# Gated cross-attention: three small regroupings of vector work, in the first quad, in every softmax and in the last two rows of tiles

## The chip, the cores and the metric

The kernel runs on one core of one Trainium2 chip. The metric is the device time of one execution in microseconds (us). The time before is 961.03 us, the median of three runs (960.99, 961.03 and 962.22).

## The reference, cut to what matters

```
memory_proj    = memory @ W_mem.T                               # (8, 64, 1024)
scores         = hidden @ memory_proj.T / sqrt(1024)            # (8, 1024, 64)
attn           = softmax(scores)
memory_context = attn @ memory_proj
gate           = sigmoid(concat(hidden, memory_context) @ W_gate.T + b_gate)
fused          = hidden + gate * memory_context
out            = fused * rsqrt(mean(fused**2) + 1e-6) * norm_w
```

Everything is float32. `hidden` is 8 x 1024 x 1024, `memory` 8 x 64 x 512, `W_gate` 1024 x 2048. The product of `hidden` with its half of `W_gate` is by far the largest piece of arithmetic.

## The kernel before, in words

**Tiling.** The 8192 rows of `hidden` are cut into 16 quads (`q`) of 512 rows; a quad is four tiles of 128 rows (`t` = 0 to 3), and each tile has two halves of 512 columns (`h` = 0, 1). Tiles 0 and 1 form row 0, tiles 2 and 3 row 1. The gate product of a quad is a two-level Strassen-like scheme: seven outer products, in `ORDER` 1, 6, 7, 5, 4, 2, 3 (the number is `o` in the code), and in each of them seven inner products. Their PSUM banks are named af, ed, kB and kC; VectorE and GpSimd add the partial sums (`u2`, `u3`, `u4`, and the "gate" tiles `O[q, t]`). The left operands need sums too: GpSimd makes them in `inner_s` (tile "l").

**Weights.** The right operands of each outer product need four sums of their own, T1, T2, R12 and T4 (`inner_sum`, tile "it"). Those of products 2 and 3 are made only once, by VectorE, within the first quad.

**Order of the work.** Everything is kept in program order on each engine. A quad has 49 slots, one per inner product. `at(slot, fn, ...)` hangs a piece of work on a slot, and `step()` issues it ahead of that slot's product; `mid((q, o), ...)` and `mid((q, o, 0), ...)` hang work in the middle of an outer product, behind and ahead of the sums that follow its visit. So each engine's queue is an order written out by hand.

**Visits.** After the third inner product of products 4 and 3 (`second` in the code), `visit` issues 32 matrix instructions for the memory half of the gate of two outer products at once, and for the attention context (tile "pc"). It takes over the banks "b" and "c", in which kB and kC had just been, so TensorE can begin only when VectorE has read kB (into `u2`) and kC (into `u3`) of the same outer product. Then `fin_af` and `fin_ed` complete the gate sums, ScalarE takes the sigmoid, and `gated` multiplies with the context.

**Softmax.** `softmax_a` (slot 10 of each quad) takes the row maximum on VectorE (L429), multiplies it there by -1/32 (L430), and ScalarE takes four exponentials (L435).

**The last quad.** There the residual comes from SBUF: `last_gated` multiplies (gate<-gate,pc) and adds `hidden` (gate<-gate,xl), `last_square` takes each half's sum of squares on ScalarE, `last_root` the square root, and `last_norm` a reciprocal (L761), one VectorE instruction that multiplies a half by the reciprocal and by `norm_w` (L765), and the store of that half from SyncE's queue (L767). `sqrt_table` loads ScalarE's table for the root ahead of need. With `slot` standing at 770 after product 4 and at 784 after product 3, the tiles of row 1 have their roots at slots 773 and 774, tile 3 its two halves at 775 and 776, tile 2 its first half in the middle of product 3 and its second at 781; all of row 0 comes after slot 784, in the order root of tile 1, root of tile 0, tile 1's halves, tile 0's halves.

Line 92 is the helper of all matmuls, line 95 that of all two-input sums, on VectorE or on GpSimd; line 98 that of SyncE's DMAs.

Of the kernel before, what the change touches and what calls it, by code (L numbers as in the profile page):

```python
# [9 lines left out]
AF = mybir.ActivationFunctionType  # L10
ALU = mybir.AluOpType
# [9 lines left out]
def tile_gated_cross_attention_rmsnorm(  # L21
# [42 lines left out]
    nc = tc.nc  # L64
# [4 lines left out]
    NQ = B * QPB  # L69
# [3 lines left out]
    H = 512  # L73
    C = 256
    NPAIR = BM // P
    SCALE = 1.0 / float(D) ** 0.5
# [12 lines left out]
    pin = tc.keep_in_program_order  # L89
# [4 lines left out]
    def tt(eng, o, a, b, op):  # L94
        pin(eng.tensor_tensor(o, a, b, op))  # L95

    def load(o, i):
        pin(nc.sync.dma_start(o, i))

    def t4k(pool, shape, tag, name):  # L100
        return pool.tile(shape, F32, tag=tag, name=name)
# [31 lines left out]
    for k in range(KD):  # L133
        t = t4k(*((gpool, [P, D], "gate") if k < 7 else (apool, [P, D], "s4")), f"w2_{k}")
# [8 lines left out]
    nw_sb = const.tile([P, D], F32, name="nw_sb")  # L143
# [194 lines left out]
    A, S, L2, O = {}, {}, {}, {}  # L338
    sTs, attns, attnTs, scs, dens, mps, mgs = {}, {}, {}, {}, {}, {}, {}
    def where(q, t=0):  # L340
        return q // QPB, (q % QPB) * QT + t * P
# [84 lines left out]
    def softmax_a(q):  # L426
        sc = scs.pop(q)
        mx = t4k(small, [P, 4], "mx", f"mx{q}")
        pin(nc.vector.tensor_reduce(mx, sc, AX.X, ALU.max))  # L429
        pin(nc.vector.tensor_scalar(mx, mx, -SCALE, None, ALU.mult))  # L430
        e = attns[q] = t4k(small, [P, 4, M], "e", f"e{q}")
        den = dens[q] = t4k(small, [P, 4], "den", f"den{q}")
        for t in range(4):
            pin(
                nc.scalar.activation(  # L435
                    e[:, t], sc[:, t], AF.Exp, bias=mx[:, t : t + 1], scale=SCALE, accum_out=den[:, t : t + 1]
                )
            )
# [167 lines left out]
    def at(slot, fn, *args):  # L606
        due.setdefault(slot, []).append(lambda: fn(*args))

    def mid(key, fn, *args):
        beside.setdefault(key, []).append(lambda: fn(*args))  # L610
# [5 lines left out]
    def plan(q):  # L616
# [11 lines left out]
        at(t0 + (11 if q else 22), outer_s, q, 4)  # L628
        at(t0 + 9, transpose_scores, q)
        at(t0 + 10, softmax_a, q)  # L630
        at(t0 + 13, softmax_b, q)
        at(t0 + 18, transpose_attn, q)
# [20 lines left out]
    for o in (2, 3):  # L653
        w1_place(o)
    for i, (o, n) in enumerate((o, n) for o in (2, 3) for n in range(4)):
        at((3, 4, 5, 6, 12, 14, 16, 18)[i], inner_sum, nc.vector, o, n)
    slot = 0

    def step():
        nonlocal slot  # L660
        for fn in due.pop(slot, ()):
            fn()
# [5 lines left out]
    def sigmoid(q, t, h):  # L668
        g = O[q, t][:, h * H : (h + 1) * H]
        pin(nc.scalar.activation(g, g, AF.Sigmoid))  # L670
# [77 lines left out]
    def last_root(t):  # L748
# [5 lines left out]
            )  # L754
        )

    def last_norm(t, h):
        b, n0 = where(NQ - 1, t)
        rstd = halves[t][0][:, 2:3]
        if h == 0:  # L760
            pin(nc.vector.reciprocal(rstd, rstd))  # L761
        cols = slice(h * H, (h + 1) * H)
        g = O[NQ - 1, t][:, cols]
        pin(
            nc.vector.scalar_tensor_tensor(g, g, rstd, nw_sb[:, cols], ALU.mult, ALU.mult)  # L765
        )
        load(out[b, n0 : n0 + P, cols], g)  # L767

    def sqrt_table():

        t = t4k(small, [P, 1], "warm", "warm")
        pin(nc.scalar.activation(t, eps_sb, AF.Sqrt))
# [75 lines left out]
    def gate(q, t, h, pc, w):  # L848
        sigmoid(q, t, h)
        if q + 1 == NQ:  # L850
            at(slot + w, last_gated, t, h, pc)
        else:
            at(slot + w, gated, q, t, h, pc)

    def outer_product(q, o):
# [4 lines left out]
        nxt = q + 1 < NQ  # L860
# [5 lines left out]
        def product(out, lhsT, s, start):  # L866
            nonlocal slot
            for k in range(2):
                mm(out, lhsT[:, k, :], w_op(o, s)[:, k, :], start and k == 0, k == 1)
            slot += 1  # L870
# [51 lines left out]
        if second:  # L922
            row, h, _ = EXT[o]
            gate(q, 2 * row + 1, h, pcs[1], 2 if o == 3 and not nxt else 1)
        step()
        product(af[:, 1], s4, R22, False)
        step()
# [8 lines left out]
        if second and not nxt:  # L936
            c, d = 2 * row, 2 * row + 1
            if o == 3:
                sqrt_table()
            when = (3, 4, 5, 6, None, 11) if o == 4 else (0, 2, 2, 2, 3, 3)  # L940
            at(slot + when[0], last_root, d)
            at(slot + when[1], last_root, c)
            for w_, (t, h_) in zip(when[2:], ((d, 0), (d, 1), (c, 0), (c, 1))):
                if w_ is None:
                    mid((q, 3, 0), last_norm, t, h_)
                else:
                    at(slot + w_, last_norm, t, h_)
        elif second:

            c, d = 2 * row, 2 * row + 1  # L950
            for t in (d, c):
                at(slot + 5, residual, q, t)
            if row == 0:
                when = (17, 18, -1, None, 33, -2) if q + 2 < NQ else (17, 18, 20, 22, 24, 25)
            else:
                when = (17, 18, 22, 24, 29, 31)
            at(slot + when[0], square, q, c)
            at(slot + when[1], square, q, d)
            for w_, (t, h_) in zip(when[2:], ((c, 0), (c, 1), (d, 0), (d, 1))):
                if w_ is None:  # L960
                    mid((q + 1, 4), norm, q, t, h_)
                elif w_ < 0:
                    mid((q + 1, 4, 0) if w_ == -1 else (q + 1, 3), norm, q, t, h_)
                else:
                    at(slot + w_, norm, q, t, h_)
        del L2[q, o]

    for q in range(NQ):
        plan(q)
        for o in ORDER:  # L970
            outer_product(q, o)
# [29 lines left out]
```

## Time and profile before

| What | Value |
|---|---|
| median of the three runs | 961.03 us |
| the profiled execution's own time | 961.78 us |
| its span in the trace | 960.0 us |
| granted TensorE clock, mean | 0.997 |
| last matrix instruction starts / span ends | 947.67 us (four of them) / 960.0 us |
| TensorE idle for VectorE's u sums, whole span | 2.2 + 0.5 + 0.2 us |
| last four stores issued at | 954.37, 955.12, 955.93 and 956.59 us |

The page gives busy time by engine. The view of waits says for whom an engine sat idle. The timeline lists instructions: start and duration in us, engine, line, operation, output and inputs with shapes, and in brackets the idle time just before and what ended it. Positions such as 941.33 are us from the span's start. The profiled execution took 0.75 us longer than the median, and its own time is 1.78 us longer than its span, so a difference is worked out on the span and then taken from either.

### The profile page before, as it was taken

To read this page: it belongs to the slowest core of one execution; us is meant where nothing else is said; L and a number is where in the kernel's file an instruction comes from. 1 tells how busy PE (TensorE), PEld (TensorE's weight loads), DVE (VectorE), ACT (ScalarE), POOL (GpSimd) and SP (SyncE) were. 2 spreads that over 40 slices of the span, in tenths; PEclk is the share of its full clock that TensorE was granted. 3 is DMA by queue.
4 is the path that set the end of the run, shared out by engine and by line. 5 is a ranking of instruction groups with operands and counts; after the bars stand their busy time and mean duration, and the time that the engine had idled before them with its cause. 6 is when DMAs were issued, how large, how long until landed. Compare 5 with 4: busy or idle time off the path is not lost.

```text
span 960.0 us, 14298 instructions
## 1 busy us (share of the span) xinstructions
PE 944.4 (98%) x4984; PEld 777.6 (81%) x4984; DVE 817.3 (85%) x1260; ACT 366.3 (38%) x779; POOL 712.2 (74%) x778
## 2 busy tenths in 40 slices
PE   9999999999999999999999999999999999999994
PEld 7546788888888888888888888888888888888883
DVE  6989878888888888988888888988888888978887
ACT  3000335262433535262433535262433525262454
POOL 4997867788677777787677777777677877777681
PEclk9999999999999999999999999999999999999998
DMA  9866674481919365481919365481919365481712
GB/s 378 268 153 155 108 126 106 104 182 44 209 45 189 91 141 118 109 177 43 210 45 189 88 142 120 101 185 40 213 45 187 87 145 121 107 180 40 203 66 89
DMA packets 70919, 128.33 MB, mean 134 GB/s; under 512 B 12352, under 2 KB 49216, under 8 KB 70592
## 3 DMA queue, kind: packets, MB, share of 16 engines
q1 hardware_dynamic: 61664, 93.86, 37.0%
q0 software_dynamic: 9184, 33.56, 19.1%
q8 instruction: 40, 0.66, 0.3%
q14 instruction: 31, 0.25, 0.1%
HBM read 87.56 MB, written 41.68 MB: 135 GB/s over the span
## 4 chain that ended last, share of the span: by engine, by line
PE 92%; DVE 4%; ACT 1%; issue 1%; POOL 1%; DMA 1%; SPq 0%; POOLq 0%; DVEq 0%; ACTq 0%
PE af L92 28%; PE ed L92 19%; PE pc L92 11%; PE kC L92 9%; PE kB L92 9%; PE psT L92 6%; PE pg L92 5%; PE pm L92 2%; DVE gate L95 1%; DVE u L95 1%; DMA wm<-in_w_mem_t 1%; POOL l L95 0%; DVE gate L765 0%; DVE gate L699 0%; PE sc L420 0%
## 5 line engine op out<-in xcount | busy, mean ns | idle before, releaser
L95 POOL TENSOR_TENSOR gate<-gate,u 128x512 f32<-128x512 f32 (+1 forms) x224 | 248.9, 1123 | 193.9 <-DVE u L95 180.0
L670 ACT ACTIVATE gate<-gate 128x512 f32<-128x512 f32 x128 | 79.8, 630 | 184.2 <-DVE gate L95 184.2
L352 DVE STREAM_TRANSPOSE a<-xq 128x512 f32<-128x512 f32 x128 | 141.0, 1105 | 3.3 <-POOL it L95 3.3
L95 POOL TENSOR_TENSOR l<-a 128x256 f32<-128x256 f32 x128 | 111.9, 874 | 18.7 <-PE af L92 17.5
L699 DVE SCALAR_TENSOR_TENSOR gate<-gate,ss,nw_sb 128x512 f32<-128x512 f32 x120 | 120.7, 1007 | 1.1
L92 PE MATMUL pc<-mg,attnT 64*128 64x256 f32 x512 | 119.0, 383 | 2.2 <-DVE u L95 2.2
L92 PE MATMUL kB<-it,l 128*128 128x256 f32 x448 | 115.1, 379 | 0.5 <-DVE u L95 0.5
L92 PE MATMUL ed<-it,l 128*128 128x256 f32 x448 | 115.0, 379 | 0.0
L92 PEld LDWEIGHTS pc<-mg,attnT 64*128 64x128 f32 x512 | 93.2, 187 | 22.9 <-DVE u L95 13.0
L876 ACT COPY u<-af 128x256 f32<-128x256 f32 x112 | 40.7, 363 | 185.6 <-PE af L92 185.2
L95 DVE TENSOR_TENSOR gate<-gate,pc 128x512 f32<-128x512 f32 x113 | 76.0, 683 | 33.2 <-ACT gate L670 33.1
L92 PE MATMUL af<-w,a 128*128 128x256 f32 x384 | 98.5, 379 | 0.0
L92 PEld LDWEIGHTS kB<-it,l 128*128 128x128 f32 x448 | 85.1, 190 | 12.3 <-issue 0.8
L92 PEld LDWEIGHTS ed<-it,l 128*128 128x128 f32 x448 | 83.9, 190 | 10.7
L95 DVE TENSOR_TENSOR gate<-gate,ed 128x512 f32<-128x512 f32 x112 | 76.1, 680 | 14.4 <-POOL gate L95 14.3
L95 POOL TENSOR_TENSOR l<-s 128x256 f32<-128x256 f32 x96 | 85.1, 886 | 3.0 <-PE af L92 3.0
L92 PEld LDWEIGHTS af<-w,a 128*128 128x128 f32 x384 | 73.0, 190 | 10.3 <-issue 0.5
L95 DVE TENSOR_TENSOR gate<-gate,af 128x512 f32<-128x512 f32 (+1 forms) x128 | 76.0, 604 | 2.1 <-POOL gate L95 1.4
L92 PE MATMUL af<-mg,attnT 64*128 64x256 f32 x256 | 68.8, 389 | 0.0
L92 PE MATMUL ed<-it,a 128*128 128x256 f32 x256 | 67.4, 386 | 0.0
L684 ACT ACTIVATE junk<-gate 128x1024 f32<-128x1024 f32 x60 | 63.5, 1058 | 6.9 <-DMA gate<-in_x 6.0
L92 PE MATMUL af<-t,s 128*128 128x256 f32 x256 | 65.8, 380 | 0.0
(138 smaller groups left out, 1993.5 us busy)
## 6 DMA issues: line engine op xcount, KB each, us to landing
xq<-in_x SPq DMA_DIRECT2D x64, 512.0 KB, 10.4
gate<-in_x POOLq DMA_DIRECT2D x60, 512.0 KB, 8.5
out<-gate SPq DMA_DIRECT2D x60, 512.0 KB, 3.4
w<-in_w_gate_t SPq DMA_DIRECT2D x8, 512.0 KB, 10.2
w<-in_w_gate_t SPq DMA_DIRECT2D x2, 2048.0 KB, 16.1
mg<-mgd SPq DMA_DIRECT2D x16, 256.0 KB, 5.9
wm<-in_w_mem_t SPq DMA_DIRECT2D x4, 512.0 KB, 6.4
mpd<-mpT SPq DMA_DIRECT2D x4, 512.0 KB, 7.0
```

What stands on the lines that cost most here:

```text
L92: pin(nc.tensor.matmul(o, lhsT, rhs, start=start, stop=stop, skip_group_check=True))
L95: pin(eng.tensor_tensor(o, a, b, op))
L352: nc.vector.transpose(A[key][:, :, r * P : (r + 1) * P], chunks(xq[q][:, 4 * t : 4 * t + 4, :], KD)[:, half * KH : (half + 1) * KH],)
L670: pin(nc.scalar.activation(g, g, AF.Sigmoid))
L684: nc.scalar.activation(junk, O[q, t], AF.Square, accum_out=ss[:, t % 2 : t % 2 + 1])
L699: nc.vector.scalar_tensor_tensor(g[:, cols], g[:, cols], rstd[:, t % 2 : t % 2 + 1], nw_sb[:, cols], ALU.mult, ALU.mult,)
L876: pin(nc.scalar.copy(p1, af[:, 0]))
```

## The change

1. In every quad, the product of the row maximum with -1/32 goes from VectorE to ScalarE, just ahead of the exponentials.
2. In the first quad, the four weight sums of outer product 3 go from slots 12, 14, 16 and 18 to the middle of product 4 (two of them, behind the gate sums of its visit), slot 33 and slot 35. Those of product 2 stay at 3 to 6.
3. In the last quad, tile 2 is multiplied by `norm_w` on GpSimd (`last_weigh`, both halves, issued in the middle of product 3), and by the reciprocal on ScalarE (slots 780 and 781). Tile 3 keeps its VectorE instructions, at slot 774 (its first half, now ahead of `u4` of product 2) and in the middle of product 3 (its second half).
4. The first halves of tiles 0 and 1 are also multiplied by `norm_w` on GpSimd, behind the last `pre` sum, and by the reciprocal on ScalarE. Their second halves stay on VectorE.

```
-        pin(nc.vector.tensor_scalar(mx, mx, -SCALE, None, ALU.mult))
+        pin(nc.scalar.activation(mx, mx, AF.Copy, scale=-SCALE))
...
-        at((3, 4, 5, 6, 12, 14, 16, 18)[i], inner_sum, nc.vector, o, n)
+        if i in (4, 5):
+            mid((0, 4), inner_sum, nc.vector, o, n)
+        else:
+            at((3, 4, 5, 6, None, None, 33, 35)[i], inner_sum, nc.vector, o, n)
...
+    def last_weigh(t, h):
+        cols = slice(h * H, (h + 1) * H)
+        g = O[NQ - 1, t][:, cols]
+        tt(nc.gpsimd, g, g, nw_sb[:, cols], ALU.mult)
...
-        pin(
-            nc.vector.scalar_tensor_tensor(g, g, rstd, nw_sb[:, cols], ALU.mult, ALU.mult)
-        )
+        if t == 2 or t < 2 and h == 0:
+            pin(nc.scalar.activation(g, g, AF.Copy, scale=rstd))
+        else:
+            pin(
+                nc.vector.scalar_tensor_tensor(g, g, rstd, nw_sb[:, cols], ALU.mult, ALU.mult)
+            )
         load(out[b, n0 : n0 + P, cols], g)
...
             gate(q, 2 * row + 1, h, pcs[1], 2 if o == 3 and not nxt else 1)
+            if o == 3 and not nxt:
+                for t in range(2):
+                    last_weigh(t, 0)
...
-            when = (3, 4, 5, 6, None, 11) if o == 4 else (0, 2, 2, 2, 3, 3)
+            when = (3, 4, 4, None, 10, 11) if o == 4 else (0, 2, 2, 2, 3, 3)
+            if o == 4:
+                for h_ in range(2):
+                    mid((q, 3, 0), last_weigh, c, h_)
```

## The prediction, made before the change was run

> **What bounds the kernel now.** I read the page's busy times first, then TensorE's waits, then the timeline around each wait and behind the last matrix instruction.
>
> ```profile
> PE 944.4 (98%) x4984; PEld 777.6 (81%) x4984; DVE 817.3 (85%) x1260; ACT 366.3 (38%) x779; POOL 712.2 (74%) x778
> PE pc L92 <- DVE u L95: 2.2, 3, 1.4
> PE kB L92 <- DVE u L95: 0.5, 1, 0.5
> PE kC L92 <- DVE u L95: 0.2, 1, 0.2
> ```
>
> TensorE is busy 98% of the span, and in all 16 quads it waits for VectorE five times. So a change to vector work can only win at those five places and behind the last matmul. Three of the five lie in the first quad:
>
> ```profile
> 109.87 1.10 PE L92 MATMUL kB<-it,l 128*128 128x256 f32 x4 [0.45 <-DVE u L95]
> 111.19 1.10 PE L92 MATMUL kC<-t,l 128*128 128x256 f32 x4 [0.21 <-DVE u L95]
> 112.75 0.48 PE L92 MATMUL pc<-mg,attnT 64*128 64x256 f32 x1 [0.46 <-DVE u L95]
> 93.63 2.23 DVE L430 TENSOR_SCALAR mx<-mx 128x4 f32<-128x4 f32 x1
> 96.70 0.84 DVE L95 TENSOR_TENSOR it<-w 128x512 f32<-128x512 f32 x1
> 103.01 0.69 DVE L95 TENSOR_TENSOR gate<-gate,ed 128x512 f32<-128x512 f32 x1 [1.51 <-POOL gate L95]
> ```
>
> The reader is to see VectorE falling behind from 93 us on: a four-column multiply that takes 2.23 us, then the weight sums, then a gate sum at 103.01 that waits for a late GpSimd. The brackets understate the loss. From af of product 4 (its last matmul group ahead of kB, 108.40) to the visit (112.75) are 4.35 us; the same stretch of product 3, without a wait, is 128.69 - 126.00 = 2.69. **The first quad loses 1.66 us.** The same subtraction in the last quad: product 4, 923.94 - 920.85 = 3.09, a loss of 0.40; product 3, 941.33 - 937.20 = 4.13, a loss of 1.44.
>
> ```profile
> 941.33 0.48 PE L92 MATMUL pc<-mg,attnT 64*128 64x256 f32 x1 [1.38 <-DVE u L95]
> 938.36 1.45 DVE L765 SCALAR_TENSOR_TENSOR gate<-gate,halves,nw_sb 128x512 f32<-128x512 f32 x1
> 941.88 1.27 POOL L95 TENSOR_TENSOR gate<-gate,u 128x512 f32<-128x512 f32 x1 [1.48 <-DVE halves L761]
> 941.91 1.79 DVE L765 SCALAR_TENSOR_TENSOR gate<-gate,halves,nw_sb 128x512 f32<-128x512 f32 x1
> 950.87 0.69 DVE L95 TENSOR_TENSOR gate<-gate,xl 128x512 f32<-128x512 f32 x1
> 954.00 0.29 ACT L752 ACTIVATE halves<-halves 128x1 f32<-128x1 f32 x1
> 955.78 0.74 DVE L765 SCALAR_TENSOR_TENSOR gate<-gate,halves,nw_sb 128x512 f32<-128x512 f32 x1
> 956.59 0.33 SPq L98 DMA_DIRECT2D out<-gate  x1
> ```
>
> Two normalising instructions stand in VectorE's queue ahead of u2, on which the last visit waits. The one at 941.91 began 0.03 us behind GpSimd's sum and took 1.79 us instead of 0.75: it ended 0.55 us after GpSimd did. So **a VectorE instruction with two SBUF inputs and a GpSimd sum exclude each other**; the one that is waiting goes next. Sums with a PSUM input keep their 0.68 us beside GpSimd (927.21). Behind the last matmul VectorE works without a pause to 956.52, and the last store, issued at 956.59, ends the span at 960.0. The four last stores move 1.05 MB from 955.2 to 958.2 at up to 385 GB/s; issued together they would need some 2.75 us.
>
> **What the Trainium skill says.** GPSIMD Engine Reference, section 8 (Key points), says that GpSimd shares its SBUF interfaces with VectorE and collides with instructions that have two SBUF inputs; the 1.79 us above agrees. The same page, section 3.1, gives some 2.6 cycles per element for a two-input GpSimd operation: my estimate for 512 columns is 512 x 2.6 / 1.2 GHz = 1.11 us, and the trace's 128x512 sums take 1.19 (back to back) to 1.27 us. ScalarE: Activation LUTs, section "Table sets: the hidden batching unit", says that a copy is in every set; the trace agrees, L876's copies run behind sigmoids, exponentials and roots without a table load. So the moved multiplies bring no load.
>
> **The change, part by part.**
>
> *Multiply of the maximum, to ScalarE.* VectorE loses 16 instructions of 0.78 us (906.74) or, in the first quad, 2.23. ScalarE gains 16 of about 0.3 us (its 128x1 operations take 0.29) in a place where it waits for the maximum anyway. In the last quad the exponentials then start some 0.55 us sooner, the reciprocal at 910.22 (which waited 0.64 for them) too, so GpSimd's and VectorE's chain up to u2 of product 4 (923.48) is about 0.6 ahead, and the loss of 0.40 goes: I take **0.35**. In the 14 quads between, TensorE waited for nothing, so it is worth nothing there; its cover is TensorE's own work.
>
> *Weight sums of product 3.* Slots 12 to 18 lose 0.84 + 0.68 + 0.69 + 0.89 = 3.10 us of VectorE, and GpSimd's left-operand sums beside them (1.17 to 1.27 us each) fall back to 0.73. Following the queue: u4 of product 7 is then ruled by TensorE (101.1), GpSimd's gate sum is done before it, and the sum of 103.01 starts at about 101.1, a lead of 1.9 us. With it u2 of product 5 is at 107.4 instead of 109.31, u3 at 108.9, and u2 of product 4 ends at about 111.0, just in time for the unstalled visit at 112.75 - 1.66 = 111.09. The same 3.1 us come back between 114 and 123 us, where VectorE has 0.43 + 0.27 + 0.69 + 0.70 us of idle time and starts 1.9 ahead; u2 of product 3 then ends within 0.2 us of the visit that needs it. Unknown is what each sum pays for colliding with GpSimd: 0.69 (no collision) to 1.84 (the worst row of a two-input instruction, 928.53). The four took 3.10 beside a busy GpSimd before, so I take that. Of 1.66 us I take **1.45**, with 0 and 1.66 as ends (TensorE is busy from there on, so what is won is kept).
>
> *Row 1 of the last quad.* u3 of product 2 stays at 937.50. The reciprocal follows at 937.83 and tile 3's first half at 938.03, 0.03 behind GpSimd's sum of 938.00, so it pays 1.79 again and ends at 939.8; u4 follows at 939.73, u2 at 940.06 to 940.47, and the visit starts at 940.53 instead of 941.33: 0.80 us of 1.44 (1.33 if VectorE came first). Tile 3's second half follows u3 (940.91) ahead of GpSimd's sum, at 0.75 us, which delays that sum to 942.75. Behind it are queued the two multiplies of tile 2, up to 943.94 and 945.13. The add of tile 0's first half (due at 944.05) waits for the second one and ends at 945.68, against 946.40 before. ScalarE's two scalings of tile 2 (0.62 each, the sigmoid's 0.61 to 0.63) fall in gaps at 944.0 and 946.7; the one removed from VectorE at 946.32 gives another 0.66. The last fin_af is at 948.18 instead of 949.55.
>
> *Row 0.* GpSimd's last gate sum ends at 948.14; its multiplies of tiles 0 and 1 run to 949.33 and 950.52. The add of tile 1's second half (due at 949.51, 950.87 before) waits for the second and ends at 951.05; tile 0's add ends at 952.38 (952.88 before). Square and root of tile 0 follow to 953.45, and only then, in ScalarE's order, come the scalings of tile 1 (953.97) and tile 0 (954.5); VectorE does the other two halves by 954.44. So the first store goes at 954.0 instead of 954.37, and, being first in SyncE's queue, it holds the others. They follow at 0.35 to 0.45 us each instead of 0.75, so the 1.05 MB need about 2.75 instead of 3.05 us. Row 0 and 1 together: 0.37 + 0.3 to 0.5, I take **0.75**. Ends: a multiply in GpSimd has no row in this trace; 1.19 (the sum's) is the floor, 2.4 (twice that) the ceiling I allow; if the adds escape both locks, 1.75.
>
> *Sum*: 0.35 + 1.45 + 0.75 = 2.55 us. The profiled execution's 961.78 becomes 959.2 (span 957.4), and the median 961.03 becomes **958.5**.
>
> **The rivals.** (a) *The first quad's loss is only moved*: the sums collide at slots 31 to 35 and hold u2 back at product 3's visit, or the lead is less than 1.2 us. Against it speaks the idle time listed above, for it the 0.2 us of slack. Then 0.35 + 0.75 remain: 959.9. (b) *The locks miss*: the adds at 944.05 and 949.51 get in ahead of GpSimd. 1.45 + 0.35 + 1.75 = 3.55: 957.5. For it: an order decided by hundredths; against: GpSimd's pairs are back to back. (c) *GpSimd's multiply is slow*, the one that ends slower than before. At 2.4 us each, tile 2's second multiply runs to about 948.1 and holds the add of tile 1's first half; fin_af comes at 949.85, tile 0's multiply to 952.2 and tile 1's to 955.15 hold the last two adds, and the first store goes at 957.4, 3.0 late. With 0.4 back from the stores and 1.8 from the other parts: 961.03 + 0.8 = 961.8. The first store moves by (3.0 + 0.37) / 1.2 = 2.8 us for each us of the multiply, so it turns slower from about 2.1 us per multiply. For it: no multiply of GpSimd in the trace; against: the skill's price is set by reading two inputs, which a sum pays too. With (a) on top it is 963.3.
>
> **How the numbers follow.** About 0.2% (1.9 us) is what a measurement here tells from no change; 959.1 and 962.95 are the bounds. Forecast 0.58 (own range 957.9 to 959.4; 0.50 of it below 959.1), (a) 0.20 (same), (b) 0.12 (faster), (c) 0.10 (0.06 slower, 0.04 same). Faster 0.62, same 0.32, slower 0.06. The range 957.2 to 960.3 takes in the forecast, (b) and (a), and leaves (c) out.
>
> **What would show it.** Right: no wait of TensorE for u between 100 and 130 us, none at product 4 of the last quad, some 0.6 us left at the last visit; GpSimd's multiplies at 1.2 us; one 1.2 to 1.8 us add in each of the two last rows; the last four stores issued within about 1.4 us. Wrong: a new wait at product 3's visit in the first quad, GpSimd multiplies near 2 us, or stores that still go one by one.

## The result and the profile after

The changed kernel takes 958.77 us (median of seven runs, 958.32 to 960.52) against 961.25 us before (median of seven): 2.5 us less, ratio 0.9974 with a 95% interval of 0.9964 to 0.9984. The prediction was 958.5. The profiled execution took 958.62 us with a span of 956.8, against 961.78 and 960.0 before: 3.2 us less, 0.7 more than the medians differ by. Where that 0.7 comes from is part of the story below.

The page's first row and TensorE's waits for VectorE's sums, after the change (us in total, times, longest):

```profile
PE 943.8 (99%) x4984; PEld 778.1 (81%) x4984; DVE 810.7 (85%) x1240; ACT 372.4 (39%) x799; POOL 719.7 (75%) x782
PE pc L92 <- DVE u L95: 0.3, 1, 0.3
```

Of five waits one is left. (A "visit" below is its first matrix instruction, the `pc<-mg,attnT` line; a bracket on it is a wait.) The timeline says which. First quad, after:

```profile
101.16 0.68 DVE L95 TENSOR_TENSOR gate<-gate,ed 128x512 f32<-128x512 f32 x1
107.43 0.42 DVE L95 TENSOR_TENSOR u<-u,kB 128x256 f32<-128x256 f32 x1
111.07 0.48 PE L92 MATMUL pc<-mg,attnT 64*128 64x256 f32 x1
114.94 0.90 DVE L95 TENSOR_TENSOR it<-w 128x512 f32<-128x512 f32 x1
115.88 1.10 DVE L95 TENSOR_TENSOR it<-w,it 128x512 f32<-128x512 f32 x1
126.40 0.39 DVE L95 TENSOR_TENSOR u<-u,kB 128x256 f32<-128x256 f32 x1
127.01 0.48 PE L92 MATMUL pc<-mg,attnT 64*128 64x256 f32 x1
```

The visit of product 4 starts at 111.07 instead of 112.75, without a bracket. Product 7's kB, which starts at 103.21 (103.22 before), is 7.86 us ahead of it instead of 9.53. The late weight sums (114.94, 115.88, and two more at 119.02 and 121.00 of 0.84 and 0.81 us) cost 3.65 us, and u2 of product 3 ends at 126.79, 0.2 us ahead of the visit that needs it.

The last quad, after: the softmax's first sum, the gate sum behind it, the visit of product 4, and then tile 2's add beside GpSimd's sum:

```profile
905.04 1.96 DVE L95 TENSOR_TENSOR s<-a,s 128x1024 f32<-128x1024 f32 x1
908.00 0.18 DVE L442 RECIPROCAL den<-den 128x4 f32<-128x4 f32 x1
913.25 0.69 DVE L95 TENSOR_TENSOR gate<-gate,ed 128x512 f32<-128x512 f32 x1 [1.13 <-POOL gate L95]
922.32 0.48 PE L92 MATMUL pc<-mg,attnT 64*128 64x256 f32 x1 [0.30 <-DVE u L95]
926.90 0.69 DVE L95 TENSOR_TENSOR gate<-gate,xl 128x512 f32<-128x512 f32 x1
926.92 1.80 POOL L95 TENSOR_TENSOR gate<-gate,u 128x512 f32<-128x512 f32 x1
938.25 0.48 PE L92 MATMUL pc<-mg,attnT 64*128 64x256 f32 x1
```

The wait that is left (0.30) is the one that I had struck out. Tile 2's add came 0.02 us ahead of GpSimd's sum here and won (0.69 us). In the first trace of before it had come 0.01 us ahead too, and lost:

```profile
928.53 1.84 DVE L95 TENSOR_TENSOR gate<-gate,xl 128x512 f32<-128x512 f32 x1
928.54 1.27 POOL L95 TENSOR_TENSOR gate<-gate,u 128x512 f32<-128x512 f32 x1
```

The starts in the trace don't tell who has the turn. That is some 0.8 us between these two profiles which no edit made (shown below), and with it the last visit (938.25) does not wait at all.

The end, after:

```profile
941.68 0.69 DVE L95 TENSOR_TENSOR gate<-gate,xl 128x512 f32<-128x512 f32 x1
943.00 1.05 DVE L95 TENSOR_TENSOR gate<-gate,xl 128x512 f32<-128x512 f32 x1
947.06 1.13 DVE L95 TENSOR_TENSOR gate<-gate,xl 128x512 f32<-128x512 f32 x1
950.30 0.29 ACT L755 ACTIVATE halves<-halves 128x1 f32<-128x1 f32 x1
950.50 1.32 ACT L773 ACTIVATE gate<-gate,halves 128x512 f32<-128x512 f32 x2
950.82 0.75 DVE L776 SCALAR_TENSOR_TENSOR gate<-gate,halves,nw_sb 128x512 f32<-128x512 f32 x1
951.23 0.33 SPq L98 DMA_DIRECT2D out<-gate  x1
```

The add of tile 0's first half (941.68) got in ahead of GpSimd and waited for nothing, where I had it wait 1.1 us; the add behind it (943.00) was held instead, for 1.05 us against 0.69 before. The add of tile 1's second half (947.06) was held, as forecast. The two scalings of ScalarE come behind tile 0's root, and the first of the last four stores goes at 951.23. From the last visit to that store are 12.98 us (13.04 before), and from it to the end 5.57 (5.63 before).

### The profile page after: what moved, and what is told of

The parts are those of the page before. It is cut to its first block, busy times and chain, and to the rows that moved or that the text cites. A ratio compares the mean times of both kernels' runs of the same rounds, so it can differ in the third digit from the quotient of the medians.

```text
span 956.8 us, 14305 instructions
## 1 busy us (share of the span) xinstructions
PE 943.8 (99%) x4984; PEld 778.1 (81%) x4984; DVE 810.7 (85%) x1240; ACT 372.4 (39%) x799; POOL 719.7 (75%) x782
## 4 chain that ended last, share of the span: by engine, by line
PE 97%; DVE 1%; DMA 1%; ACT 0%; issue 0%; POOL 0%; SPq 0%; ACTq 0%; DVEq 0%
PE af L92 30%; PE ed L92 21%; PE pc L92 12%; PE kC L92 10%; PE kB L92 10%; PE psT L92 6%; PE pg L92 5%; PE pm L92 2%; DMA wm<-in_w_mem_t 1%; PE pa L451 0%; PE sc L420 0%; DVE gate L702 0%; DVE u L95 0%; DVE gate L95 0%; ACT junk L743 0%
## 5 line engine op out<-in xcount | busy, mean ns | idle before, releaser
L95 POOL TENSOR_TENSOR gate<-gate,u 128x512 f32<-128x512 f32 (+1 forms) x224 | 243.1, 1098 | 184.5 <-DVE u L95 148.6
L702 DVE SCALAR_TENSOR_TENSOR gate<-gate,ss,nw_sb 128x512 f32<-128x512 f32 x120 | 115.4, 963 | 1.1
L95 POOL TENSOR_TENSOR l<-s 128x256 f32<-128x256 f32 x96 | 78.5, 818 | 3.0 <-PE af L92 3.0
L95 DVE TENSOR_TENSOR u<-u,kC 128x256 f32<-128x256 f32 x112 | 45.9, 410 | 23.8 <-PE kC L92 20.3
```

The source lines that it names most:

```text
L702: nc.vector.scalar_tensor_tensor(g[:, cols], g[:, cols], rstd[:, t % 2 : t % 2 + 1], nw_sb[:, cols], ALU.mult, ALU.mult,)
```

## The experiments

Each execution starts differently: kB of product 7 in the first quad comes at 103.16 to 104.68 us in the twelve traces besides the first two (103.21 and 103.22). So spans of single executions aren't compared, but stretches: from that kB to the visit of product 4 (first quad), from one visit to the next in the last quad, and from the last visit to the end. The spans are given to 0.1 us, so a stretch that ends with the span is good to about 0.05. The times come from rounds beside the kernel before on the same chip.

**The multiply of the maximum alone**, in the kernel before:

```
-        pin(nc.vector.tensor_scalar(mx, mx, -SCALE, None, ALU.mult))
+        pin(nc.scalar.activation(mx, mx, AF.Copy, scale=-SCALE))
```

> The kernel before with the multiply of the row maximum on ScalarE alone. My prediction gave it 0.35 us (the wait at product 4's visit in the last quad gone): 960.9 against 961.25. The theory read from the trace after: the lead of 0.6 us at the softmax's reciprocal is used up by sums that collide with GpSimd, so nothing (within 0.1 us) is left at that visit, and the wait of 0.3 us stays. A second question is whether the add of tile 2's second half, which met a GpSimd sum within 0.02 us in both traces, gets in first (0.7 us) or second (1.8 us).

Measured: 961.69 us against 962.27, ratio 0.9994 (0.9987 to 1.0000). Its trace, product 4's visit in the last quad and tile 2's add:

```profile
923.56 0.48 PE L92 MATMUL pc<-mg,attnT 64*128 64x256 f32 x1 [0.29 <-DVE u L95]
928.14 0.69 DVE L95 TENSOR_TENSOR gate<-gate,xl 128x512 f32<-128x512 f32 x1
928.16 1.81 POOL L95 TENSOR_TENSOR gate<-gate,u 128x512 f32<-128x512 f32 x1
```

The wait stays at 0.29 (0.34 before), so the gain that I had named isn't there. VectorE came first at the add here too. The first quad's stretch is 9.24 us; the kernel before has 9.53 in one trace and 9.10 in another, so nothing is seen of this part there either. Between the two quads, from product 3's visit at 128.35 to 923.56, are 795.21 us, against 795.25 in the kernel before. If it is worth anything (the time allows 0 to 1.25 us), no trace shows where.

The kernel before shows why. In the last quad:

```profile
905.84 1.65 POOL L95 TENSOR_TENSOR gate<-gate,u 128x512 f32<-128x512 f32 x1 [0.83 <-issue]
906.74 0.78 DVE L430 TENSOR_SCALAR mx<-mx 128x4 f32<-128x4 f32 x1
907.44 1.21 DVE L95 TENSOR_TENSOR s<-a,s 128x1024 f32<-128x1024 f32 x1
914.87 0.69 DVE L95 TENSOR_TENSOR gate<-gate,ed 128x512 f32<-128x512 f32 x1 [0.84 <-POOL gate L95]
```

The multiply ends at 907.52, 0.03 us behind GpSimd's sum. In all four traces that have it on VectorE (the kernel before twice, the sums alone, the rows alone) all 64 of these multiplies end 0.01 to 0.05 us behind a GpSimd sum, whether they took 0.78 us or 2.28; on ScalarE the same multiply takes 0.21. So nearly all of its time on VectorE was a wait for GpSimd, and with the multiply gone the next sum takes the wait over (1.96 us at 905.04 in the changed kernel, instead of 1.21).

**The weight sums alone**, in the kernel before:

```
-        at((3, 4, 5, 6, 12, 14, 16, 18)[i], inner_sum, nc.vector, o, n)
+        if i in (4, 5):
+            mid((0, 4), inner_sum, nc.vector, o, n)
+        else:
+            at((3, 4, 5, 6, None, None, 33, 35)[i], inner_sum, nc.vector, o, n)
```

> The kernel before with the weight sums of product 3 at their late places alone (multiply of the maximum still on VectorE). Theory: the three waits of the first quad go and 1.66 us are kept to the end: 959.6 against 961.25. Rival: the lead of 1.9 us came in part from the multiply of the maximum (2.23 us in the first quad); without its move some of the waits stay and the gain is 0.5 to 1.2 us.

Measured: 960.47 against 962.27, ratio 0.9981 (0.9974 to 0.9987): 1.8 us less. The first quad's stretch is 111.87 - 104.01 = 7.86 us, the same as with all parts (111.07 - 103.21 = 7.86). The sums do this alone.

```profile
104.01 1.03 PE L92 MATMUL kB<-it,l 128*128 128x256 f32 x4
111.87 0.48 PE L92 MATMUL pc<-mg,attnT 64*128 64x256 f32 x1
```

With GpSimd first at tile 2's add in this trace, the last visit waits as in the kernel before:

```profile
PE pc L92 <- DVE u L95: 1.7, 2, 1.4
```

**The two rows of the last quad alone**: the changed kernel with the multiply and the sums as before, so that parts 3 and 4 are left.

```
-        pin(nc.scalar.activation(mx, mx, AF.Copy, scale=-SCALE))
+        pin(nc.vector.tensor_scalar(mx, mx, -SCALE, None, ALU.mult))
...
-        if i in (4, 5):
-            mid((0, 4), inner_sum, nc.vector, o, n)
-        else:
-            at((3, 4, 5, 6, None, None, 33, 35)[i], inner_sum, nc.vector, o, n)
+        at((3, 4, 5, 6, 12, 14, 16, 18)[i], inner_sum, nc.vector, o, n)
```

> The kernel before with the changes to the last quad's normalising alone. Theory (my prediction's terms for both rows): 0.75 us less, 960.5, with the last visit 0.8 us sooner. Rival from the trace after: that part and the order of the add and GpSimd's sum belong together, 1.5 us less, 959.7.

Measured: 961.16 against 962.27, ratio 0.9988 (0.9981 to 0.9996): 1.1 us less (0.4 to 1.8), between the two expectations; the interval takes in both. Its trace decides for the first one: VectorE came first at tile 2's add (929.00, 0.69 us), and from product 4's visit to the end are 958.9 - 924.42 = 34.48 us, 0.78 less than in the kernel before with the same order (35.26, its second trace, below).

**Without part 4**, twice, the second time beside the changed kernel itself:

```
-            if o == 3 and not nxt:
-                for t in range(2):
-                    last_weigh(t, 0)
...
-        if t == 2 or t < 2 and h == 0:
+        if t == 2:
```

> The changed kernel without its part 4: the first halves of tiles 0 and 1 are normalised by VectorE as before. If part 4 is worth nothing because the last four stores are bound by how fast 1.05 MB flows from the first of them on, and the first one is no sooner with it than without: within 0.2 us of 958.77. If the saving of two VectorE instructions at the end counts: 0.7 us slower, 959.5. If GpSimd's two multiplies cost more by holding VectorE's add (1.13 instead of 0.69 us) than they bring: 0.4 us faster, 958.4.

> The changed kernel without part 4, once more, beside the changed kernel. Theory from its first trace: part 4 costs 0.65 us (0.44 for the add that GpSimd's multiply holds, the rest for a first store that waits for ScalarE behind tile 0's root), so this is 0.65 us faster than the changed kernel. My prediction's working: part 4 is a small gain, so this is 0.2 to 0.7 us slower.

> The changed kernel once more, to be timed beside the three others. If the order of tile 2's add and GpSimd's sum (0.02 us apart in every trace so far) is chance, this profile shows either one; with VectorE first the add takes 0.7 us and the last visit does not wait, with GpSimd first it takes 1.8 us and the last visit waits about 0.6 us. Median as before: 2.5 us under the kernel before, give or take 0.5.

Measured: first 958.89 against 962.27, ratio 0.9959 (0.9946 to 0.9973); the second time, beside the changed kernel, 958.69 against its 959.41, with 961.90 for the kernel before: ratios 0.9966 (0.9953 to 0.9978) and 0.9973 (0.9961 to 0.9984). The intervals overlap, and the two profiled executions of the second time don't help: they are 0.77 us apart (958.66 and 959.43), but 0.74 of it lies ahead of product 7's kB (103.36 and 104.10), and from product 4's visit to the end both need 34.5 to 34.6 us, since GpSimd came first at tile 2's add in the one and VectorE in the other. Behind the last visit the traces are clear. Without part 4, second trace:

```profile
938.96 0.48 PE L92 MATMUL pc<-mg,attnT 64*128 64x256 f32 x1 [0.57 <-DVE u L95]
947.76 0.69 DVE L95 TENSOR_TENSOR gate<-gate,xl 128x512 f32<-128x512 f32 x1
950.48 1.41 DVE L776 SCALAR_TENSOR_TENSOR gate<-gate,halves,nw_sb 128x512 f32<-128x512 f32 x2
951.26 0.33 SPq L98 DMA_DIRECT2D out<-gate  x1
```

From the last visit to the end it needs 956.9 - 938.96 = 17.94 us; the changed kernel 18.55 and, again, 957.7 - 939.06 = 18.64. The add is not held (0.69 instead of 1.13), and the first store goes 951.26 - 938.96 = 12.30 us behind the visit instead of 12.98. **From the last visit on, part 4 costs about 0.65 us**: 18.55 to 18.65 us in the four traces with parts 3 and 4 as they stand, 17.9 to 18.0 in the three with part 3 alone. My working had made it a part of a gain. Both traces without part 4 had GpSimd first at tile 2's add; there the last visit waits 0.57 and 0.58, the 0.6 us that my prediction, worked out on a trace with that order, left there.

**The order of the last stores**, in the changed kernel (tiles 1 and 0: second half ahead of the first):

```
-        if h == 0:
+        if h == (1 if t < 2 else 0):
             pin(nc.vector.reciprocal(rstd, rstd))
...
-            for w_, (t, h_) in zip(when[2:], ((d, 0), (d, 1), (c, 0), (c, 1))):
+            f_ = 1 if o == 3 else 0
+            for w_, (t, h_) in zip(when[2:], ((d, f_), (d, 1 - f_), (c, f_), (c, 1 - f_))):
```

> The changed kernel with the last four stores in another order: of tiles 1 and 0 the second half, which VectorE finishes, is stored ahead of the first, which ScalarE finishes. Nothing else moves. If the end is set by the first store and by how fast 1.05 MB flows from it on, the first store goes 0.7 us sooner and the end comes 0.6 us sooner than in the changed kernel. If the end is set by the last multiply and its own store, nothing changes (0 to 0.1 us).

Measured: 958.60 against 959.41 of the changed kernel beside it (ratio to the kernel before 0.9965, 0.9952 to 0.9977). In its trace the last multiplies end when they did, the first store goes sooner:

```profile
938.89 0.48 PE L92 MATMUL pc<-mg,attnT 64*128 64x256 f32 x1
950.40 0.75 DVE L776 SCALAR_TENSOR_TENSOR gate<-gate,halves,nw_sb 128x512 f32<-128x512 f32 x1
951.13 1.32 ACT L773 ACTIVATE gate<-gate,halves 128x512 f32<-128x512 f32 x2
951.18 0.33 SPq L98 DMA_DIRECT2D out<-gate  x1
```

951.18 - 938.89 = 12.29 us from visit to first store, 0.69 less than the changed kernel's 12.98, and 956.8 - 938.89 = 17.91 to the end, 0.64 less. No arithmetic was saved: **the end follows the first store**, not the last multiply. Without part 4 VectorE's last multiply ends 0.9 us later behind the visit than here (953.41 - 938.96 = 14.45 us against 952.45 - 938.89 = 13.56), and the end comes at the same distance (17.94 and 17.91). The run also tells what part 4's 0.65 us are. Tile 1's add is held here as in the changed kernel (947.69, 1.13 us), and yet the first store is as early as without part 4. ScalarE squares that half only at 949.14, behind its table load, when the add has already ended (948.82). So the held add costs nothing here, and the whole 0.65 is the first store's wait for ScalarE.

**A second GpSimd multiply ahead of each of the four** (of `norm_w` with itself, into a tile that nobody reads; 1.04 us where nothing holds it):

```
+        spare = t4k(small, [P, H], "pe", f"spare{t}_{h}")
+        tt(nc.gpsimd, spare, nw_sb[:, cols], nw_sb[:, cols], ALU.mult)
         tt(nc.gpsimd, g, g, nw_sb[:, cols], ALU.mult)
```

> The changed kernel with a second GpSimd multiply of the same size (128x512, two SBUF inputs, into a spare tile that nobody reads) ahead of each of the four. It prices the rival of a slow GpSimd multiply. If GpSimd holds VectorE's adds and its own last gate sum queues behind the multiplies: fin_af waits 1.4 us longer for that sum, the two last adds collide, the first of the last stores goes 2.5 us later and the end comes 2.0 to 2.8 us later than in the changed kernel. If GpSimd is off the path: 0 to 0.3 us later.

Measured: 961.93 against 961.56, ratio 1.0001 (0.9992 to 1.0009): the whole gain of the change is lost. From the last visit (939.55) to the first store (955.01) are 15.46 us, 2.48 more than in the changed kernel:

```profile
942.78 1.26 POOL L95 TENSOR_TENSOR gate<-gate,nw_sb 128x512 f32<-128x512 f32 x1
942.98 1.61 DVE L95 TENSOR_TENSOR gate<-gate,xl 128x512 f32<-128x512 f32 x1
945.45 1.72 POOL L95 TENSOR_TENSOR gate<-gate,nw_sb 128x512 f32<-128x512 f32 x1
950.14 1.48 DVE L95 TENSOR_TENSOR gate<-gate,xl 128x512 f32<-128x512 f32 x1
```

So the mechanism of my slow rival is there, at the size of the expectation and a little under that of the prediction (2.4 us at the first store for each us of GpSimd, instead of 2.8). What kept it away is that a GpSimd multiply takes 1.26 to 1.27 us where nothing holds it (942.78 here, 940.53 and 945.15 in the changed kernel), the same as a sum.

**The race at tile 2's add.** One trace more of each of two kernels, without an edit, of the kernel before and of the multiply alone:

> The kernel before once more, for its trace: which of tile 2's add and GpSimd's sum comes first. In the first trace GpSimd did (0.01 us apart). If the order belongs to the program, GpSimd again; if it is chance, either.

> The kernel with the moved multiply of the maximum alone, once more, for its trace: VectorE came first in its first trace. If the order belongs to the program, VectorE again; if it is chance, either.

The kernel before, second trace:

```profile
923.54 0.48 PE L92 MATMUL pc<-mg,attnT 64*128 64x256 f32 x1 [0.34 <-DVE u L95]
928.13 0.69 DVE L95 TENSOR_TENSOR gate<-gate,xl 128x512 f32<-128x512 f32 x1
928.15 1.80 POOL L95 TENSOR_TENSOR gate<-gate,u 128x512 f32<-128x512 f32 x1
940.15 0.48 PE L92 MATMUL pc<-mg,attnT 64*128 64x256 f32 x1 [0.60 <-DVE u L95]
```

VectorE came first, where in the first trace GpSimd had. It is the same program, so no edit made the order; what does is not known, and it is called chance here. From one visit to the other this execution needs 940.15 - 923.54 = 16.61 us, the first 941.33 - 923.94 = 17.39: **0.78 us by chance.** The multiply alone had VectorE first again (928.95, 0.69 us). So the change's own gain is read from traces with the same order: with VectorE first in both, 16.61 and 15.93 us between the two visits, so 0.68; with GpSimd first in both, 17.39 and 16.59 (924.01 to 940.60, first trace without part 4), so 0.80. Of the twelve traces in which the two can meet like this, GpSimd came first in five and VectorE in seven. How often either comes first in the timed executions isn't on record.

**Taking the race away**: GpSimd's gate sum of product 4 ahead of the last two left-operand sums, in the last quad only, once without part 4 and once with it:

```
-                    at(t0 + 7 * i + t, inner_s, q, ORDER[i + 1], part)
+                    late = not nxt and i == 4 and part == 1
+                    at(t0 + 7 * i + (3 if late else t), inner_s, q, ORDER[i + 1], part)
```

> The changed kernel without part 4, and in the last quad GpSimd adds the gate sum of product 4 (128x512) ahead of the last two left-operand sums of product 2 instead of behind them. If the order of tile 2's add and that gate sum costs 0.8 us in the executions in which GpSimd comes first, the add now collides with a short sum at most (0.0 to 0.7 us of wait), the last visit waits less than 0.6 us, and the median is 0.2 to 0.5 us under the kernel without part 4. If the race is of no account, it is the same within 0.1 us; if the two sums that now come later hold TensorE, it is slower.

> The changed kernel, part 4 included, with GpSimd's gate sum of product 4 ahead of the last two left-operand sums in the last quad, as in the run of that name without part 4. With the race taken away from both, the two differ by part 4 alone: theory 0.65 us slower than that run (0.9967 of the kernel before against 0.9960), rival: the same within 0.2 us, and the earlier difference was the race.

Measured: without part 4, 958.03 us beside 961.90, ratio 0.9960 (0.9948 to 0.9973), the lowest median of all: 1.4 us under the changed kernel and 0.66 under the same kernel with the race. The intervals overlap, and without part 4 the first ratio had been 0.9959, so the times alone don't rank them. With part 4, 958.71 beside 961.56, ratio 0.9970 (0.9959 to 0.9981). Without part 4:

```profile
925.81 1.27 POOL L95 TENSOR_TENSOR gate<-gate,u 128x512 f32<-128x512 f32 x1
927.04 0.73 POOL L95 TENSOR_TENSOR l<-a 128x256 f32<-128x256 f32 x1
927.16 1.15 DVE L95 TENSOR_TENSOR gate<-gate,xl 128x512 f32<-128x512 f32 x1
938.51 0.48 PE L92 MATMUL pc<-mg,attnT 64*128 64x256 f32 x1
```

The add now meets a short sum and pays 1.15 us, and the last visit doesn't wait: from visit to visit are 938.51 - 922.57 = 15.94 us, what the race gives with VectorE first. So this edit takes the bad case away and doesn't better the good one. From the last visit to the end are 956.5 - 938.51 = 17.99 us, and with part 4 957.6 - 938.95 = 18.65: part 4's 0.66 once more, with the race out of both.

## Why the prediction was right, step by step

**First quad: right.** Forecast and measured agree nearly to the hundredth: the gate sum at 101.1 (101.16), u2 of product 5 at 107.4 (107.43), the visit at 111.09 (111.07). The late sums cost 3.65 us instead of the 3.10 that I took, and the idle time took that up. I had put 1.45 us to it; the trace shows 1.67 against the first trace of before, 1.24 against the second, in which the multiply of the maximum had waited less for GpSimd (1.78 us instead of 2.23), and 1.74 against the rows alone (9.60, with 2.28); timed alone it is 1.8 (1.25 to 2.5). Rival (a) is refuted by the visits' missing waits.

**Multiply of the maximum: the step that failed.** "GpSimd's and VectorE's chain up to u2 of product 4 is about 0.6 ahead" is not so. The lead of 0.6 is there at the reciprocal (908.00 against 910.22, where the kernel runs 1.62 ahead), and it is gone at 913.25, which is exactly 1.62 ahead of 914.87. The reading that failed is that of the multiply's 0.78 us as work, when it was a wait for GpSimd: VectorE's 1024-column sum took the wait over (1.96 instead of 1.21 us). The reciprocal did come sooner, because the exponentials did. But GpSimd's queue stayed where it was, so VectorE waited 1.13 us for its gate sum instead of 0.84, and two of GpSimd's left-operand sums met VectorE (1.22 and 1.18), where one had before. A lead on one engine was paid back to the other, and of my 0.35 us the traces show 0.03 to 0.05 (the wait of 0.34 is 0.29 to 0.31 wherever the multiply is moved).

**Row 1 and row 0: the sum right, the parts not.** I had 0.80 at the last visit, and the measured 0.68 to 0.80 is that. From the visit to the first store I had 0.43 us lost; measured 0.06 won, 0.49 better. The add of tile 0's first half came 0.08 us ahead of GpSimd's second multiply (941.68 against 941.76) instead of 0.11 behind it (944.05 against 943.94). So GpSimd's last gate sum ended 6.94 us behind the visit instead of 7.61, the multiplies after it came sooner too, and the add of tile 1's second half, forecast at 1.54 us, took 1.13. From the first store to the end I had 0.3 to 0.5 us won, since four stores in close order "need about 2.75 instead of 3.05 us"; measured 0.06 between the two profiles, which is the rounding of the span. This step is wrong: in all fourteen traces, with 1.7 to 2.2 us from the first to the last issue, first store to end is 5.57 to 5.69 us (5.63 before; 5.57 and 5.67 changed; 5.69 with the doubled multiply). Together 0.74 to 0.86 instead of 0.75; the rows alone, timed, 1.1 (0.4 to 1.8).

**What the rows hide.** I costed them as one, and they are a gain and a loss: with part 3 alone the stretch from the last visit to the end is 17.9 us instead of 18.67, and part 4 gives 0.65 of that back. It saves VectorE two instructions at a point where VectorE is no longer what the end waits for, and makes the first store wait for ScalarE's scaling behind tile 0's root, which it had not needed before.

**Sum.** From the traces, 1.24 to 1.74, next to nothing and 0.74 to 0.86 are 2.0 to 2.6 us; timed 2.5 (1.5 to 3.5); forecast 2.55. Two steps promised too much, by 0.35 and about 0.4, and the collision that did not happen gave 0.49 back. That the sum came out so close is in part luck. Rival (b), at 957.5, had both adds of VectorE get in ahead of GpSimd; one did, the other did not. Rival (c) was refuted by the 1.27 us of the multiply and, as a mechanism, borne out by its double. Of the signs that I had named for being right, the first quad's missing waits and the multiplies at 1.2 us came. The wait at product 4 stayed, the one at the last visit was 0 instead of 0.6 in this trace, the two held adds took 1.05 and 1.13 us instead of 1.2 to 1.8, and the stores were issued within 1.69 us instead of 1.4.

## What to carry to other kernels

Before an instruction is moved off a busy engine, look at what its time is made of. If it ends each time just behind an instruction of the other engine, it is waiting, and the next one may wait in its place, as it did here. When VectorE and GpSimd share work as here, write the two queues side by side and see who is in front at each place where they can exclude each other; a lead on one alone is not yet a gain. An order that was decided by hundredths of a microsecond fell either way in two executions of one program; look for it before crediting a change with what luck gave, and reorder so that it can't matter. At the end of a kernel, ask which store goes first, and let nothing slow stand ahead of it.

## What the runs showed of the hardware that was not expected

- The race: VectorE's add starts 0.01 to 0.03 us ahead of GpSimd's sum in all twelve of these traces, and either can have the turn: GpSimd at 928.53 and 928.54 (first trace of before) and at 927.55 and 927.58 (doubled multiply), and VectorE at 928.13 and 928.15 (second trace of before). The loser waits for the whole instruction of the other: 1.84 against 0.69 us for VectorE, 1.80 against 1.27 for GpSimd.
- VectorE's four-column multiply has a single SBUF input and was held by GpSimd all the same: 64 of 64 ended 0.01 to 0.05 us behind a GpSimd sum. In the first quad it waited past two of them (93.63 for 2.23 us, kernel before, beside GpSimd's sums at 93.60 and 94.28), so "the one that is waiting goes next", which the prediction read from larger instructions, doesn't hold for it. A 128x1 reciprocal in the midst of a GpSimd sum (938.16, beside 938.00, kernel before) took 0.16 us and was not held.
- The end of the four last stores keeps its distance from the first issue (5.57 to 5.69 us in fourteen traces), whether the last is issued 1.7 or 2.2 us behind it. Why is open.
- The second of the last stores was issued 0.75 us behind the first (951.23 and 951.98) though its data had been there since 950.52; the third and fourth followed at 0.45 and 0.49. What holds the second is open; it wasn't tried.
- ScalarE's scaling of a 128x512 half by one number per partition takes 0.70 to 0.72 us in the changed kernel, where its sigmoid of the same size takes 0.61 to 0.63.
